# A four-layer network on one core: first loads on two queues, the bias split moved, layer 1's bands prepared in other tiles, q (k^T v) taken two head pairs at a time

## The chip, the cores and the metric

The kernel runs on one NeuronCore of one Trainium2 chip. The metric is the device time of one execution in microseconds (us), lower is better, as the median of several executions. Engines are named as the profile names them: PE is TensorE, DVE VectorE, ACT ScalarE, POOL GpSimd, SP SyncE, which here only issues DMAs. PEld is TensorE's loading of weights, which overlaps its matmuls.

## The reference

The input x has the shape (4, 8, 512, 512): time T, batch B, rows N, columns D. Four layers follow one another, each a residual on a group normalisation of x (two batch entries make one group):

```python
x = x + attention(_gn(x), ...)   # layer 0
x = x + conv13x13(_gn(x), w)     # layer 1, one Gaussian kernel per channel, reflected edges
x = x + conv3x3_quantised(_gn(x), weight, bias)   # layer 2
x = x + conv3x3(_gn(x), weight, bias)             # layer 3
```

Layer 0, where the change lies, is a spiking attention with 8 heads of 64 columns:

```python
q = heads(lif(bn(x @ Wq.T)))     # the same for k and v
scores = einsum('tbhnd,tbhmd->tbhnm', q, k) * scale + bias_table[rel]
out = lif(einsum('tbhnm,tbhmd->tbhnd', scores, v))
out = lif(bn((out * gate_scale + gate_shift) @ Wp.T))
```

`lif` runs over the four time steps: a potential is averaged with its input, gives a spike (0 or 1) where it reaches 1, and is then reset. No softmax stands between scores and values. So scores @ v may be taken as q (k^T v), which needs only a 64 x 64 matrix for each head, plus the bias matrix times v. The bias depends on the distance of two rows alone.

## The kernel before

**Layer 0** (`layer0`, L268 to L733) goes through 32 steps, one for each (b, t). What a step needs of the projections is made one step ahead. In the loop over n, `attend` (L533) works on step n, then `project_in` (L518) makes v, k and q of step n+1, in 3 x 4 groups, and `project_out` (L579) for step n is put between them in four groups.

- `attend`: k^T v goes into one PSUM tile (L540) and is cut to the heads' diagonal blocks on DVE as `kvb` (L545). Then, for each pair of heads j = 0 to 3: `pa` = q·kvb (L552, two matmuls of 64 output rows) and `pb` = the bias times v (L560, 24 matmuls, since the bias is kept as three bf16 parts and the 512 rows are contracted in four blocks of 128). Potential and spikes follow on DVE (ACT in the first time step). The spikes of all four pairs, the tile `so`, feed `project_out`.
- `project_in`: a group is four program matmuls in f32, eight instructions. Its PSUM tile is emptied by DVE into potential and spikes.
- PSUM tiles: the pool `ps_mm` has four that projections in and out and small products share; `ps_b` has two for pb; `ps_1` has one for pa and one for k^T v and small sums.

**The start.** ACT issues `cols` (batch norm parameters) and `bias_table`; SP issues the first x in four quarters (`xq`, L447), a second x of the same group (`xs`, L438), then the weights of v, k and q in quarters (L308). A group's statistics are made on DVE from both x (L456), summed over partitions by small matmuls (`gps`, L180), and normalise xq, which is then transposed (L505). The weights are scaled on DVE by the batch norm's factors (L359), which PE has spread over the free axis (`ps_free`, L346). Then the first v projection runs.

**Prologue.** Beside the projections of step 0 the kernel prepares what later work needs. `split_bias` (L364) splits the bias table into three bf16 parts on DVE and writes them to DRAM. `prepare_bias` (L380) reads them back as 12 hankel tiles, 448 KB each, over ACT's queue, and ACT turns each into a part of `toep`. `prepare_out` (L401) makes the output weights; it needs the `shift` matmuls (L407). `bands1` (L736) prepares layer 1's band matrix in a scratch tile that takes over a buffer of the pool `state` ("h_p"): it fills the DRAM tensor `band1d` with zeros from SBUF (one DMA, 896 KB by the page), computes 13-wide bands by four matmuls (L769) from the constants `c13` and the taps `w1`, writes them into band1d, and sums the taps by a matmul with ones (L784). The ones are written over the zeros (L782).

**Order.** The program is written in Python order, and a scheduler orders the instructions of each engine by its own estimate of times, within dependencies and the hints `tc.issue_after(op)`. An engine carries out its instructions in that order. A tile's buffer is given to the next tile of the same tag once its readers are done. A DMA from SP or ACT takes one of eight semaphores in turn, and so waits for the DMA eight earlier, whichever of the two queues that was on.

**After layer 0** come layer 1 (`Layer1`, L810) with one band matmul a tile (L843), and layers 2 and 3 (L1037).

Of the kernel before, what the change touches and what calls it, by code (L numbers as in the profile page):

```python
# [35 lines left out]
F32 = mybir.dt.float32  # L36
# [6 lines left out]
PSUM = bass.MemoryType.PSUM  # L43

P = 128
T, B, N, D, H = 4, 8, 512, 512, 8
DH = D // H
NC = N // P
SQ = 32
# [8 lines left out]
PH, NV = 4, D // 4  # L58
W1_IN, W1_OUT = 28, 16
W1_N = N // W1_OUT  # L60
X1_R, X1_U = N + 2 * R1, (D + 2 * R1) // PH
# [68 lines left out]
def network(ctx: ExitStack, tc: tile.TileContext, i: dict, out: bass.AP):  # L130
    nc = tc.nc
# [96 lines left out]
            s, tc, i, x_in, x1d, ident, block, avg, group_stats, st1, norm1, band1d, r1, w_sum, shared  # L228
        )

    nc.vector.tensor_scalar_mul(avg_same, same, 1.0 / n_half)

    def pool(name, bufs=1, **where):
        return tc.tile_pool(name=name, bufs=bufs, reuse_waits="tile", **where)

# [10 lines left out]
    with ExitStack() as s:  # L246
        ps_1 = s.enter_context(pool("ps_2", space=PSUM))
        layer1 = Layer1(
            s, tc, x1d, x2d, avg, group_steps, r1, mr1, st2, m2, r2, most, w_sum, head, ps_1, pool
        )  # L250
        layer1.group(0)
        for g in range(1, G):
            if g == 1:
                with ExitStack() as behind:
                    for op in layer1.started:
                        behind.enter_context(tc.issue_after(op))
                    norm1(G - 1, ps_1)
# [10 lines left out]
def layer0(  # L268
# [2 lines left out]
    nc = tc.nc  # L271
    half_scale = 0.5 / math.sqrt(D)

    ps_mm = s.enter_context(tc.tile_pool(name="ps_mm", bufs=4, space=PSUM))
    ps_b = s.enter_context(tc.tile_pool(name="ps_b", bufs=2, space=PSUM))
    ps_1 = s.enter_context(tc.tile_pool(name="ps_1", bufs=1, space=PSUM))
    wpool = s.enter_context(tc.tile_pool(name="w0", bufs=1))
# [24 lines left out]
    work = s.enter_context(tc.tile_pool(name="work", bufs=1))  # L302


    def load_weights(n, engine):
        rows = i[f"wT_{n}"].rearrange("(q c a) e -> q a c e", c=NC, a=SQ)
        for q in range(P // SQ):
            engine.dma_start(wT[n][q * SQ : (q + 1) * SQ], rows[q])  # L308

    nc.scalar.dma_start(cols.rearrange("p a b -> p (a b)"), i["cols"])  # L310
    bn = cols[:, :16, :].rearrange("p (n s) c -> p n s c", s=4)
# [52 lines left out]
    def split_bias():  # L364

        n_e = n_h // 3
        parts = tc.dram_tile([3, H * n_h], BF16, name="bias_parts")
        src = state.tile([3 * H, n_e], F32, tag="h_o", name="bias_table")
        nc.scalar.dma_start(src, bass.AP(i["table"].tensor, 0, [[n_e, 3 * H], [1, n_e]]))
        part = state.tile([3 * H, 3, n_e], BF16, tag="h_p", name="bias_part")  # L370
        for z in range(3):
            nc.vector.tensor_copy(part[:, z, :], src)
            if z < 2:
                nc.vector.tensor_sub(src, src, part[:, z, :])
        nc.scalar.dma_start(
            bass.AP(parts.tensor, parts.offset, [[n_e, 3 * H], [H * n_h, 3], [1, n_e]]), part
        )
        return parts
# [60 lines left out]
            got.append(xt)  # L439
        return got  # L440

    def load_quarters(b, t):

        xt = xqp.tile([P, N // SQ, P], F32, tag="xq", name=f"xq_{b}_{t}")
        rows = x_in[t, b].rearrange("(j s) (q f) -> q s j f", s=SQ, f=P)
        for q in range(P // SQ):
            nc.sync.dma_start(xt[q * SQ : (q + 1) * SQ], rows[q])  # L447
        return xt

    def as_rows(xt):  # L450
# [82 lines left out]
    def attend(got, t):  # L533
        q, k, v = got["q"], got["k"], got["v"]

        kv = ps_1.tile([P, NC, P], F32, tag="misc", name="ps_kv")
        for j in range(NC):
            cut = slice(j * P, (j + 1) * P)
            for c in range(NC):
                nc.tensor.matmul(  # L540
                    kv[:, j, :], lhsT=k[:, c, cut], rhs=v[:, c, cut],
                    start=c == 0, stop=c == NC - 1,
                )
        kvb = work.tile([P, NC, P], F16, tag="kvb", name="kvb")
        nc.vector.tensor_mul(kvb, kv, block.unsqueeze(1).to_broadcast([P, NC, P]))  # L545
        spikes = work.tile([P, NC, N], F32R, tag="so", name="so")
        for j in range(NC):
            pa = ps_1.tile([P, N], F32, tag="pa", name="ps_a")
            pb = ps_b.tile([P, N], F32, tag="pb", name="ps_b")
            for two in range(2):  # L550
                out = slice(two * DH, (two + 1) * DH)
                nc.tensor.matmul(  # L552
                    pa[out, :], lhsT=kvb[:, j, out], rhs=q[:, j, :], start=True, stop=True
                )
            for c in range(NC):
                u = P * (NC - 1 - c)
                for z in range(3):
                    for two in range(2):
                        h = 2 * j + two
                        nc.tensor.matmul(  # L560
                            pb[two * DH : (two + 1) * DH, :],
                            lhsT=v[:, c, h * DH : (h + 1) * DH],
                            rhs=toep[z][:, h, u : u + N],
                            start=c == 0 and z == 0,
                            stop=c == NC - 1 and z == 2,
                        )
# [8 lines left out]
            nc.vector.scalar_tensor_tensor(w, pb, 0.5, w, op0=ALU.mult, op1=ALU.add)  # L575
            fire(w, h, t, None, spikes[:, j, :])
        return spikes
# [70 lines left out]
    def load(n):  # L648
        if n <= last:
            xs[n] = load_quarters(*steps[n])  # L650
# [18 lines left out]
    a_rows = as_rows_of(a_half.rearrange("p n c -> p (n c)"))  # L669
    c_rows = as_rows_of(c_half[:, :3, :].rearrange("p n c -> p (n c)"))  # L670
    with tc.issue_after(normed):
        load(0)
        statistics(0, 0, 0, as_rows(xs[0]))
        statistics(0, 0, 1, load_x(1, 0, "xs"))
        for n in "vkq":
            load_weights(n, nc.sync)
        bias_parts = split_bias()
    for k in range(NC):
        transpose(0, k)
# [3 lines left out]
    for n in range(-1, last + 1):  # L683
# [39 lines left out]
        if n < 0:  # L723
            with ExitStack() as behind:
                for op in first:
                    behind.enter_context(tc.issue_after(op))
                prepare_bias(bias_parts)
                prepare_out(load_out())
                next_group(n)
                bands1(tc, i, band1d, w_sum, eye, ps_mm, state)  # L730
            for name in "op":
                h_of[name] = state.tile([P, NC, N], F32, tag=f"h_{name}", name=f"h_{name}")
    return head  # L733


def bands1(tc, i, band1d, w_sum, eye, psum, state):  # L736


    nc = tc.nc
    n_s = SHIFTS * PH  # L740
    n_w, n_p = K1 + 2 * (PH - 1), K1 * PH
    scratch = state.tile([P, 2 * P + B * n_w + PH * n_p + B], F32, tag="h_p", name="bands1")
    at = 0

    def part(n_part, n):
        nonlocal at
        at += n
        return scratch[:n_part, at - n : at]
# [14 lines left out]
    nc.vector.memset(zeros, 0.0)  # L763
    rest = band1d.rearrange("p (r m) -> p r m", r=W1_OUT)
    nc.scalar.dma_start(rest, zeros.unsqueeze(1).to_broadcast([K1_P, W1_OUT, P]))

    ps = psum.tile([n_p, P], F32, tag="mm", name="ps_band")
    for f in range(PH):
        nc.tensor.matmul(  # L769
            ps, lhsT=c13[:, f, :], rhs=w1[:, :, f : f + n_s], start=f == 0, stop=f == PH - 1  # L770
        )
# [10 lines left out]
    nc.vector.memset(zeros[:K1, :], 1.0)  # L782
# [565 lines left out]
```

## Time and profile before

| | us |
|---|---|
| three executions | 2902.84, 2903.57, 2905.07 (median 2903.57) |
| the profiled execution | 2902.63 |
| its span, first to last instruction | 2900.8 |
| mean granted TensorE clock | 0.991 |
| layer 0 | from 0 to about 2024 |
| layer 1 | to about 2483 |
| layers 2 and 3 | to 2896 |

Layer 0's steps, from one first v matmul to the next: 81.5 us for the first (with the prologue), 64.2 and 66.2 for the next two, then 61.3 to 63.4. Where DVE's kvb came too late for PE in later steps, PE waited 1.22 us at 718, 0.81 at 1150, 1.71 at 1214 and under 0.6 twice more.

The page is to be read so: busy times are sums over the whole span and say which engine is full; the groups say which line holds the time, and behind the bar how long the engine had been idle just before and on whom it waited. The timeline gives the start of a run of like instructions, its length, and in brackets the idle time ahead of it with its releaser. `ACTq` and `SPq` are the issuing of DMAs; the data moves later.

### The profile page before, as it was taken

The numbers are of one execution on the slowest core, as the hardware profiler recorded it, in microseconds if no ns is written. First come the engines' busy times: TensorE is split into PE (matmuls) and PEld (weight loads), VectorE is DVE, ScalarE is ACT, GpSimd is POOL, SyncE is SP. The second block draws the span as 40 slices with busy tenths as digits, with TensorE's granted clock in tenths as the row PEclk, the third lists the DMA queues.
The fourth block names the chain that finished last, engine by engine and source line by source line (L and its number), as shares of the span: only waits on it lengthen the run. The fifth ranks groups of instructions, "written<-read, shape, count | busy, mean of one in ns | idle before, by whom it ended". The sixth has DMA issues, their size and how long they took to land. (4 is left out here: it accounts for less than half of the span.)

```text
span 2900.8 us, 36559 instructions
## 1 busy us (share of the span) xinstructions
PE 2818.8 (97%) x12868; PEld 1302.5 (45%) x12868; DVE 2183.1 (75%) x3888; ACT 549.2 (19%) x851; POOL 868.8 (30%) x1920
## 2 busy tenths in 40 slices
PE   7999999999999999999999999999999999689999
PEld 3444555545555545455555555445333333223334
DVE  6897788788779878878877886886665665888870
ACT  2200100011010001001000000110111121677774
POOL 2242243333234323333422343332311111232220
PEclk9899999999999999999999999999999999999999
DMA  8433222223222232222222122212877788699975
GB/s 209 115 89 76 59 67 67 74 74 74 59 67 67 77 76 68 59 67 67 75 67 51 45 59 52 52 45 75 221 203 207 209 219 224 157 201 234 224 191 148
DMA packets 326127, 324.01 MB, mean 112 GB/s; under 512 B 21519, under 2 KB 240439, under 8 KB 325831
## 3 DMA queue, kind: packets, MB, share of 16 engines
q1 hardware_dynamic: 263024, 239.48, 34.1%
q0 software_dynamic: 19776, 56.14, 6.0%
q10 hardware_dynamic: 43143, 26.05, 3.1%
q8 instruction: 101, 1.65, 0.3%
q14 instruction: 83, 0.68, 0.1%
HBM read 212.44 MB, written 103.65 MB: 109 GB/s over the span
## 5 line engine op out<-in xcount | busy, mean ns | idle before, releaser
L524 PE MATMUL ps_in<-w_v,xn 128*128 128x512 f32 x1024 | 459.1, 599 | 5.4 <-DVE w_v L359 5.4
L524 PE MATMUL ps_in<-w_kq,xn 128*128 128x512 f32 x1024 | 449.8, 592 | 0.0
L843 PE MATMUL ps_conv<-x,bt 112*64 112x512 f32 x2048 | 445.2, 592 | 0.1
L524 PE MATMUL ps_in<-xn,w_kq 128*128 128x512 f32 x1024 | 444.9, 592 | 0.0
L560 PE MATMUL ps_b<-toep,vtok 128*64 128x512 bf16 x3072 | 367.1, 383 | 0.4 <-DVE v_o L575 0.4
L475 ACT ACTIVATE h_q<-v_q,c_half 128x512 f32<-128x512 f32 x96 | 69.1, 721 | 1473.6 <-DVE v_q L471 893.9
L500 POOL TENSOR_TENSOR h_v<-h_v,c_v 128x512 f32<-128x512 f32 x96 | 121.8, 1269 | 728.0 <-DVE h_v L499 700.1
L587 PE MATMUL ps_out<-wp,so 128*128 128x512 f32 x1024 | 308.7, 444 | 0.0
L609 POOL COPY x1s<-x1s 128x2 f32<-128x2 f32 (+1 forms) x1024 | 226.6, 275 | 273.0 <-DVE x1s L598 273.0
L524 PEld LDWEIGHTS ps_in<-xn,w_kq 128*128 128x128 f32 x1024 | 194.3, 190 | 232.5 <-issue 220.4
L524 PEld LDWEIGHTS ps_in<-w_kq,xn 128*128 128x128 f32 x1024 | 194.3, 190 | 220.7 <-issue 206.2
L524 PEld LDWEIGHTS ps_in<-w_v,xn 128*128 128x128 f32 x1024 | 191.4, 191 | 222.9 <-issue 212.1
L843 PEld LDWEIGHTS ps_conv<-x,bt 112*64 112x64 f32 x2048 | 146.5, 135 | 288.0 <-issue 286.0
L560 PEld LDWEIGHTS <-vtok 128*64 128x64 bf16 x3072 | 176.1, 111 | 155.1 <-issue 5.6
L1249 PE MATMUL ps_conv<-x,band_t 64*64 64x512 f32 x2040 | 242.7, 595 | 0.0
L587 PEld LDWEIGHTS ps_out<-wp,so 128*128 128x128 f32 x1024 | 192.6, 188 | 94.0 <-issue 57.8
L1153 DVE SCALAR_TENSOR_TENSOR x<-ps_conv,inv,x 128x512 f32<-128x512 f32 (+1 forms) x172 | 186.1, 1169 | 46.9 <-PE ps_conv L1146 46.7
L598 DVE SCALAR_TENSOR_TENSOR x1s<-v_p,xr 128x256 f32<-128x256 f32 x256 | 187.6, 773 | 14.6 <-DMA x<-x1s 3.8
L865 POOL DMA_DIRECT2D x<-xo x128 | 71.4, 564 | 330.6 <-ACT xo L850 316.3
L850 ACT ACTIVATE xo<-ps_conv,off 128x512 f32<-128x512 f32 x128 | 87.6, 687 | 430.6 <-PE ps_conv L843 307.4
L500 POOL TENSOR_TENSOR h_k<-h_k,c_k 128x512 f32<-128x512 f32 x96 | 122.0, 1270 | 138.4 <-DVE h_k L499 138.4
L1146 PE MATMUL ps_conv<-xq,band 128*128 128x512 bf16 (+1 forms) x516 | 131.5, 391 | 31.3 <-POOL xq L1129 31.3
(193 smaller groups left out, 3113.8 us busy)
## 6 DMA issues: line engine op xcount, KB each, us to landing
x<-x SPq DMA_DIRECT2D x64, 917.0 KB
x<-x SPq DMA_DIRECT2D x168, 256.0 KB
x<-x1s POOLq DMA_DIRECT2D x128, 262.0 KB, 2.7
xq<-in_x SPq DMA_DIRECT2D x128, 256.0 KB
xr<-in_x SPq DMA_DIRECT2D x128, 256.0 KB
out<-o SPq DMA_DIRECT2D x164, 192.0 KB
xs<-in_x SPq DMA_DIRECT2D x112, 256.0 KB
x<-xo ACTq DMA_DIRECT2D x128, 128.0 KB
```

The lines of the kernel that those rows point to most:

```text
L500: nc.gpsimd.tensor_add(h, h, c_twice[n])
L524: mm = nc.tensor.matmul(ps, lhsT=lhsT, rhs=rhs, start=k == 0, stop=k == NC - 1)
L560: nc.tensor.matmul(pb[two * DH : (two + 1) * DH, :], lhsT=v[:, c, h * DH : (h + 1) * DH], rhs=toep[z][:, h, u : u + N], start=c == 0 and z ...
L587: nc.tensor.matmul(ps, lhsT=so[:, k, c * P : (c + 1) * P], rhs=wpT[z][:, k, :], start=k == 0 and z == 0, stop=k == NC - 1 and z == 1,)
L598: nc.vector.scalar_tensor_tensor(own, v.rearrange("p (g v) -> p g v", g=PH)[:, two, :], 1.0, by_phase[:, two, :], op0=ALU.is_ge, op1=ALU.add,)
L609: nc.gpsimd.tensor_copy(x1[:, f, u : u + n], x1[:, fm, um - n + 1 : um + 1][:, ::-1])
L843: mm = nc.tensor.matmul(ps[q * M1 : (q + 1) * M1, :], lhsT=bt[:, z, :], rhs=xt[:, w0 : w0 + N_PS1, z : z + NV], start=z == 0, stop=z == SH ...
L850: nc.scalar.activation(xo[:, a, :], ps, AF.Identity, bias=off[:, t : t + 1])
L865: engine.dma_start(bass.AP(dst.tensor, dst.offset + (q * n_half * W1_OUT * B + b) * D + f * NV, [[B * D, W1_OUT], [W1_OUT * B * D, n_half] ...
L1146: mm = nc.tensor.matmul(ps[:n_p, :], lhsT=w["band2"][:n_p, j, dx, :n_p], rhs=xq[:, j, dx : dx + PH, :], start=dx == 0, stop=dx == 2,)
L1153: done["DVE"] = nc.vector.scalar_tensor_tensor(own.rearrange("p (v g) -> p g v", g=PH), by_phase(ps[:n_p, :]), w["inv"][:n_p], by_phase(x[ ...
L1249: mm = nc.tensor.matmul(ps[j][b * HALF : (b + 1) * HALF, :], lhsT=band[half, b, dx, :], rhs=x3[half, s0 + j, dx : dx + D], start=dx == 0, ...
```

## The change

- First loads: the quarters 2 and 3 of the first x, and of the weights of v, are issued by ACT; k and q stay on SP. ACT issues `bias_table` behind them.
- The bias split: the three casts go to ACT, the two subtractions to POOL.
- `bands1`: its scratch is a tile of `x1p` (layer 0's output tiles, two buffers), the zeros have the other of the two, and `c13` and the taps are loaded by POOL's queue. It no longer waits for the buffer "h_p".
- `attend`: pa of two pairs of heads is taken one after the other, each behind the last bias matmul of the pairs before (for j = 0 and 1 behind k^T v's last). pa has two PSUM tiles, `ps_mm` three.
- `avg_same`, one scaling of a constant, is made ahead of layer 1's second group.

```diff
@@ network
-    nc.vector.tensor_scalar_mul(avg_same, same, 1.0 / n_half)
...
                     for op in layer1.started:
                         behind.enter_context(tc.issue_after(op))
+                    nc.vector.tensor_scalar_mul(avg_same, same, 1.0 / n_half)
                     norm1(G - 1, ps_1)
@@ layer0
-    ps_mm = s.enter_context(tc.tile_pool(name="ps_mm", bufs=4, space=PSUM))
+    ps_mm = s.enter_context(tc.tile_pool(name="ps_mm", bufs=3, space=PSUM))
@@ load_weights and load_quarters, each with a parameter engines
-            engine.dma_start(wT[n][q * SQ : (q + 1) * SQ], rows[q])
+            engines[q // 2].dma_start(wT[n][q * SQ : (q + 1) * SQ], rows[q])
...
-            nc.sync.dma_start(xt[q * SQ : (q + 1) * SQ], rows[q])
+            engines[q // 2].dma_start(xt[q * SQ : (q + 1) * SQ], rows[q])
@@ split_bias
-            nc.vector.tensor_copy(part[:, z, :], src)
+            nc.scalar.copy(part[:, z, :], src)
             if z < 2:
-                nc.vector.tensor_sub(src, src, part[:, z, :])
+                nc.gpsimd.tensor_sub(src, src, part[:, z, :])
@@ attend
-        for j in range(NC):
-            pa = ps_1.tile([P, N], F32, tag="pa", name="ps_a")
-            pb = ps_b.tile([P, N], F32, tag="pb", name="ps_b")
+
+        def through_kv(j):
+            pa = ps_1.tile([P, N], F32, tag="pa", name="ps_a", bufs=2)
             for two in range(2):
                 out = slice(two * DH, (two + 1) * DH)
                 nc.tensor.matmul(
                     pa[out, :], lhsT=kvb[:, j, out], rhs=q[:, j, :], start=True, stop=True
                 )
+            return pa
+
+        for j in range(NC):
+            if j % 2 == 0:
+                with tc.issue_after(mm.ins):
+                    pas = [through_kv(jj) for jj in (j, j + 1)]
+            pa = pas[j % 2]
+            pb = ps_b.tile([P, N], F32, tag="pb", name="ps_b")
@@ layer0's first loads
-        load(0)
+
+        both = nc.sync, nc.scalar
+        xs[0] = load_quarters(*steps[0], both)
         statistics(0, 0, 0, as_rows(xs[0]))
         statistics(0, 0, 1, load_x(1, 0, "xs"))
-        for n in "vkq":
-            load_weights(n, nc.sync)
+        load_weights("v", both)
+        for n in "kq":
+            load_weights(n, (nc.sync, nc.sync))
         bias_parts = split_bias()
...
-                bands1(tc, i, band1d, w_sum, eye, ps_mm, state)
+                bands1(tc, i, band1d, w_sum, eye, ps_mm, x1p)
@@ bands1
-    scratch = state.tile([P, 2 * P + B * n_w + PH * n_p + B], F32, tag="h_p", name="bands1")
+    scratch = pool.tile([P, PH, X1_U], F32, tag="x1", name="bands1").rearrange("p f u -> p (f u)")
+    zeros = pool.tile([P, PH, X1_U], F32, tag="x1", name="zeros1")
+    zeros = zeros.rearrange("p f u -> p (f u)")[:K1_P, :P]
-    zeros, band = part(K1_P, P), part(n_p, P)
+    band = part(n_p, P)
-    nc.scalar.dma_start(
+    nc.gpsimd.dma_start(
         c13, i["c13"].rearrange("k (f j) -> k f j", f=PH)[:, :, (W1_OUT - 1) * PH :][:, :, :n_p]
     )
-    nc.scalar.dma_start(taps, i["w1"].rearrange("k (c d) -> k c d", c=B))
+    nc.gpsimd.dma_start(taps, i["w1"].rearrange("k (c d) -> k c d", c=B))
```

More of the change, by code (lines that the diff above doesn't have):

```diff
@@ L302, in layer0, with load_weights @@
     work = s.enter_context(tc.tile_pool(name="work", bufs=1))
-    def load_weights(n, engine):
+    def load_weights(n, engines):
         rows = i[f"wT_{n}"].rearrange("(q c a) e -> q a c e", c=NC, a=SQ)
         for q in range(P // SQ):
-            engine.dma_start(wT[n][q * SQ : (q + 1) * SQ], rows[q])
+            engines[q // 2].dma_start(wT[n][q * SQ : (q + 1) * SQ], rows[q])
     nc.scalar.dma_start(cols.rearrange("p a b -> p (a b)"), i["cols"])
@@ L440, in load_x, with load_quarters @@
         return got
-    def load_quarters(b, t):
+    def load_quarters(b, t, engines=(nc.sync, nc.sync)):
         xt = xqp.tile([P, N // SQ, P], F32, tag="xq", name=f"xq_{b}_{t}")
@@ L539, in attend @@
             for c in range(NC):
-                nc.tensor.matmul(
+                mm = nc.tensor.matmul(
                     kv[:, j, :], lhsT=k[:, c, cut], rhs=v[:, c, cut],
@@ L559, in attend @@
                         h = 2 * j + two
-                        nc.tensor.matmul(
+                        mm = nc.tensor.matmul(
                             pb[two * DH : (two + 1) * DH, :],
@@ L733, in layer0, with bands1 @@
     return head
-def bands1(tc, i, band1d, w_sum, eye, psum, state):
+def bands1(tc, i, band1d, w_sum, eye, psum, pool):
     nc = tc.nc
```

## The prediction

> **What bounds the kernel now.** I read the page's engine table first, then the groups by line with their shapes kept apart, then the busy times by stretch, and last the timeline of each stretch that lost something.
>
> ```profile
> PE 2818.8 (97%) x12868; PEld 1302.5 (45%) x12868; DVE 2183.1 (75%) x3888; ACT 549.2 (19%) x851; POOL 868.8 (30%) x1920
> L552 PE MATMUL ps_a<-q,kvb 128*64 128x512 f16 x256 | 55.8, 393 | 11.7 <-DVE kvb L545 10.5
> ```
>
> TensorE is the bound: it is idle for 2900.8 − 2818.8 = 82 us in all. So the change can win only idle time, half-clock time or matmul time; it removes no matmul. The second line says that q·kvb, which the change regroups, waited 10.5 us for kvb over all 32 steps.
>
> ```profile
> 0.00:23.00 23.00, 5.99 (x23) 5.00 (x24) 14.16 (x37) 2.39 (x4) 4.95 (x9) 1.00 0.88 195
> 69.00:104.00 35.00, 28.69 (x181) 18.20 (x181) 23.39 (x43) 15.94 (x23) 0.54 (x1) 0.71 0.55 141
> 104.00:168.00 64.00, 62.80 (x257) 31.51 (x256) 58.94 (x110) 5.45 (x9) 25.86 (x50) 1.00 0.39 100
> 168.00:234.00 66.00, 63.11 (x256) 31.53 (x252) 58.90 (x102) 5.41 (x8) 25.71 (x49) 0.97 0.30 81
> 234.00:296.00 62.00, 61.97 (x256) 31.32 (x252) 44.08 (x78) 1.26 (x2) 15.50 (x41) 1.00 0.28 69
> ```
>
> Columns: length, then PE, PEld, DVE, ACT and POOL busy, the clock, DMA share, GB/s. Layer 0's regular step (last row) leaves TensorE no hole. What can be had lies in the start (17 us idle), the prologue of step 0 (6.3 us idle at clock 0.71) and the first two steps (1.2 and 2.9 us idle, with VectorE busy 59 of 64 to 66 us: it sets their length). The other 50 us or so are in layers 1 to 3, which the change hardly touches.
>
> ```profile
> 22.66 5.94 PE L524 MATMUL ps_in<-w_v,xn 128*128 128x512 f32 x8 [5.35 <-DVE w_v L359]
> ...
> 89.68 0.64 PE L552 MATMUL ps_a<-q,kvb 128*64 128x512 f16 x2 [2.33 <-DVE kvb L545]
> 93.87 1.91 PE L769 MATMUL ps_band<-bands 13*52 13x128 f32 x8 [3.56 <-DMA bands<-in_w]
> 96.75 1.01 PE L560 MATMUL ps_b<-toep,vtok 128*64 128x512 bf16 x3 [0.41 <-DVE v_o L575]
> ...
> 158.06 1.89 PE L560 MATMUL ps_b<-toep,vtok 128*64 128x512 bf16 x16
> 159.78 0.38 PE L552 MATMUL ps_a<-q,kvb 128*64 128x512 f16 x2
> 160.00 2.76 PE L560 MATMUL ps_b<-toep,vtok 128*64 128x512 bf16 x24
> 162.59 0.38 PE L552 MATMUL ps_a<-q,kvb 128*64 128x512 f16 x2
> ...
> 222.48 0.64 PE L552 MATMUL ps_a<-q,kvb 128*64 128x512 f16 x2 [2.89 <-DVE kvb L545]
> 222.91 3.02 PE L560 MATMUL ps_b<-toep,vtok 128*64 128x512 bf16 x16
> ```
>
> **What the Trainium skill says.** "TensorE: Matmul & The Clock Gate", Part 1, has TensorE run at half clock by default and after an idle window of about 3.4 us, until it has been busy as long again. The trace agrees in kind, already for shorter waits: after the 2.89 us at 222.48 sixteen matmuls took 225.76 − 222.91 = 2.85 us, at 158.06 they took 1.72, so the wait cost 1.1 us more than itself. "DMA: Bandwidth & Descriptors", section "Issuing engines are not separate DMA queues", says a second issuing engine saves only the time of issuing. The trace agrees that little else is to be had: the DMA engines are at 0.88 in the first 23 us. The same page's "Queues, rings and completion order" has descriptors of one ring consumed in order; that places the zeros transfer below behind the hankels. "GPSIMD Engine Reference", 4.1, makes a two-input operation about twice VectorE's time; no 24x341 subtraction of GpSimd is in the trace.
>
> **1. Start.** From VectorE go three casts and two subtractions.
>
> ```profile
> 7.75 0.32 DVE L372 CAST bias_part<-bias_table 24x341 bf16<-24x341 f32 x1
> 9.94 2.48 DVE L456 BATCH_NORM_STATS2 st<-xq 128x6 f32<-128x512 f32 x4
> 12.33 2.46 DVE L456 BATCH_NORM_STATS2 st<-xs 128x6 f32<-128x512 f32 x4
> ```
>
> They fill 7.75 to 9.87, ahead of the statistics on which everything to the first matmul (22.66) hangs. If xs is there, the whole 2.1 us are won; the last xs quarter landed at about 11.7 now, and the statistics take it in fourths of 0.62, so at worst 1.5 us are. I take 1.75. The split goes to ScalarE and GpSimd (two subtractions at an estimated 1.0 us, twice 0.50), later than now, but its first reader, a hankel, is issued only at 30.68: hidden. w_v's third and fourth quarters go by ScalarE's queue; their landing (18.6 at the latest) is ahead of the scaling at 21.95 already: nothing.
>
> **2. The zeros transfer, a new wait.** band1d is first filled with zeros, a transfer of 896 KB.
>
> ```profile
> 92.81 0.69 ACTq L765 DMA_DIRECT2D band1d<-bands  x1
> 98.70 0.17 DVE L782 MEMSET bands<- 13x128 f32 x1 [0.92 <-DMA band1d<-bands]
> ```
>
> With its own tile it is issued much earlier, in ScalarE's order right behind the sixth hankel pair, at about 48. The memset that rewrites the zeros with ones then stands on VectorE before k's last potential, and it waits until the transfer has read them. VectorE works in order. Behind the memset stand k's last potential and spikes (1.75 us), the statistics of the next x (8 x 0.61 = 4.84), q's first potential (0.7) and the sum (0.2): 7.5 us, with one wait more 7.75. TensorE asks for that sum now after eleven of q's sixteen matmuls (two instructions of 0.43 us each) in place of thirteen: 65.88 − 1.72 − 1.75, about 62.4. The hankels ahead in the queue had their data from 49 to 55.9; the zeros took 4.0 us alone (94 to 98), so they land between 55 (shared from the start) and 59.5 (wholly behind). I take 58.4: the sum is ready at 66.15 and TensorE waits 3.75, then loses some 1.6 to half clock (1.3 to 2.3 by the case at 222). From 54.5 downwards it would cost nothing.
>
> **3. kvb and the bands in step 0.** kvb's multiply stands on VectorE ahead of the output weights' chain, no longer late behind it: 2.33 goes. c13 and the taps come over GpSimd's queue some 60 us before they are used: 3.56 goes. The 0.41 goes too, with some 0.7 of q·kvb that stretched to 95.71–96.75, and half clock after those waits (89.7 to 98.8), about 1.9. Sum 8.9. The change puts v's two groups for step 1 (6.87 us) into this place as filler; so the first ps_out follows straight on the last bias matmul and needs the last spikes: of b3's 0.69, comparison and write 0.42, and the drain, about 2.0 us of wait. The scaling rows move behind the shift matmuls: they delay the output weights by 1.4 us, which the bias matmuls (7 us at 77) cover.
>
> **4. Steps 1 and 2.** They are VectorE's; it can be early only by its own lead (0.7 to 3 us) and by the waits for TensorE it loses (up to 2.3). Of a gain up to 5 all can pass, of more than that not.
>
> **5. q·kvb by fours, three PSUM tiles.** In a regular step a pair of q·kvb takes 160.00 − 159.78 = 0.22 us, and 24 bias matmuls take 2.59, 0.216 a pair: switching between them costs nothing, so doing it half as often saves nothing. The first q·kvb still stands behind eight bias matmuls and waits for kvb as now. For the bank that the second q·kvb takes, the projections give one up. Over the 512 projection groups of this trace, comparing when VectorE or ScalarE emptied a tile with when the matmul three groups on began, none would have waited: the least slack is 0.27 us with three (4.09 with four). I put it at 0, with 0.1 us a step (3 us) as bound.
>
> **6. avg_same** (0.26 us at 6.83, beside GpSimd's 2.94 us power): 0.
>
> Sum: −1.75 + 3.75 + 1.6 − 8.9 + 2.0 = −3.3 us. The profiled execution took 2902.63 (span 2900.8 and 1.8 around it), 0.9 under the median; so 2899.3 for such a run, and against the median 2903.57 − 3.3 = **2900.3 us**. Ends of the single terms: start −1.5 to −2.1, the zeros 0 to 7.3, step 0 −6 to −7 net.
>
> **Rivals.** *The zeros land early.* If they share the engines with the hankels and land by 54.5, part 2 falls away: −1.75 − 6.9 = −8.65, of which VectorE in steps 1 and 2 may keep 1: **2895.5**. For it: DMA share is 0.81 before 69. Against: one queue, in order, behind 0.9 MB.
> *Three PSUM tiles stall the projections* (the slower side). The slack of 0.27 us is from one step; VectorE's busy steps (53.7 of 61 us) recur. A wait of 0.3 us in each of 31 steps gives −3.3 + 9.3 = +6.0: **2909.6**. It decides from 3.3/31, about 0.11 us a step. For it: drains lag by up to 6.4 us, and three tiles hold 3 x 3.43 us. Against: no group of the trace overlaps.
> *The regrouping pays.* If pairs in fours saved 0.2 us a step, −3.3 − 6.2: **2894.1**. The 0.22 above speaks against.
>
> **How the numbers follow.** My forecast 0.60, early zeros 0.24, PSUM 0.12, regrouping 0.04. What a measurement can tell from no change is 0.2%, 5.8 us: faster means below 2897.8, slower above 2909.4. The forecast's own range, 2896.5 to 2904.5, lies nearly all within it (0.55 of its 0.60), PSUM half. So faster 0.05 + 0.24 − 0.02 + 0.04 = 0.31, slower 0.08, same 0.61. The range 2894 to 2907 leaves out PSUM's worse half and the tail of early zeros, about 0.17.
>
> **What would show it.** Right: the first v matmul at 20.6 to 21.2 in place of 22.66; a VectorE memset near 52 waiting for the transfer of band1d, and TensorE's gps waiting some 4 us near 62 to 66; no wait of 2.33 and 3.56 around 90, one of some 2 us at the first ps_out; regular steps of the same 61.5 us. Wrong: steps of other length (PSUM or regrouping), a gps without a wait (early zeros), or a step 1 that ends no earlier although step 0 does.

## The result and the profile after

The changed kernel takes 2909.14 us (median of 20 runs, 2903.61 to 2912.69). The kernel before took 2903.51 on the same chip (20 runs, 2900.90 to 2905.71). The ratio is 1.0018, with a 95% interval of 1.0012 to 1.0025: 5.6 us slower, where 3.3 us faster was forecast and the range ended at 2907. The profiled execution took 2907.84 us, its span 4.9 us longer than before.

The engine line of the page and the busy times by stretch, for the kernel after. The columns are those of the same view before. The last three rows lie inside the rows above them.

```profile
PE 2816.4 (97%) x12868; PEld 1298.1 (45%) x12868; DVE 2188.5 (75%) x3883; ACT 549.4 (19%) x854; POOL 872.9 (30%) x1924
```

```profile
0.00:23.00 23.00, 5.65 (x22) 4.66 (x22) 10.85 (x28) 3.82 (x7) 7.42 (x12) 1.00 0.99 213
...
69.00:104.00 35.00, 34.77 (x207) 19.24 (x206) 25.68 (x47) 18.41 (x25) 0.67 (x1) 0.91 0.46 131
104.00:168.00 64.00, 55.24 (x205) 26.17 (x205) 58.82 (x104) 4.78 (x7) 28.22 (x50) 0.97 0.39 100
...
234.00:296.00 62.00, 61.97 (x258) 31.44 (x256) 44.78 (x81) 1.89 (x3) 15.51 (x41) 1.00 0.27 69
...
120.00:140.00 20.00, 19.08 (x55) 9.21 (x52) 20.00 (x35) 0.00 (x0) 15.23 (x27) 1.00 0.27 81
160.00:168.00 8.00, 7.83 (x58) 3.85 (x60) 5.17 (x10) 1.35 (x2) 0.00 (x0) 0.79 0.70 123
224.00:230.00 6.00, 3.88 (x24) 1.83 (x26) 4.02 (x8) 1.29 (x2) 0.00 (x0) 0.72 0.82 155
```

TensorE's matmuls cost the same (2816.4 us busy against 2818.8); its idle time grew from 82.0 to 89.3 us. The stretch from 69 to 104, which was to be won, was won: TensorE is busy 34.77 of 35 us at clock 0.91, before 28.69 at 0.71. The next one was lost: 55.24 of 64, before 62.80. VectorE is as busy there as before (58.82), and from 120 to 140 it has no hole at all. The regular step has not moved.

TensorE's timeline after (start, duration, operation, and in brackets the wait ahead of it and what ended it):

```profile
24.36 2.93 PE L523 MATMUL ps_in<-w_v,xn 128*128 128x512 f32 x3 [5.84 <-DVE w_v L358]
...
67.42 0.38 PE L180 MATMUL gps_x<-gsum_x,avg 128*128 128x1 f32 x2 [2.13 <-DVE gsum_x L177]
...
103.58 1.67 PE L594 MATMUL ps_out<-wp,so 128*128 128x512 f32 x6
106.05 0.74 PE L594 MATMUL ps_out<-wp,so 128*128 128x512 f32 x2 [0.80 <-DVE so L468]
107.84 3.70 PE L523 MATMUL ps_in<-w_v,xn 128*128 128x512 f32 x8 [1.05 <-DVE v_v L491]
...
160.17 0.62 PE L551 MATMUL ps_a<-q,kvb 128*64 128x512 f16 x4 [3.80 <-DVE kvb L544]
...
226.12 1.07 PE L551 MATMUL ps_a<-q,kvb 128*64 128x512 f16 x4 [2.74 <-DVE kvb L544]
...
2570.82 1.46 PE L1158 MATMUL ps_conv<-xq,band 128*128 128x512 bf16 x6 [1.92 <-POOL xq L1141]
...
2589.16 1.46 PE L1158 MATMUL ps_conv<-xq,band 128*128 128x512 bf16 x6 [1.73 <-POOL xq L1141]
```

And VectorE's, then ScalarE's, after:

```profile
11.15 2.47 DVE L455 BATCH_NORM_STATS2 st<-xq 128x6 f32<-128x512 f32 x4 [3.45 <-DMA xq<-in_x]
...
60.05 0.17 DVE L794 MEMSET zeros<- 13x128 f32 x1 [5.84 <-DMA band1d<-zeros]
...
95.94 1.29 DVE L430 TENSOR_TENSOR wp_k<-wp_k,wp 128x512 f32<-128x512 f32 x2 [3.92 <-ACT wp L429]
```

```profile
51.13 0.69 ACTq L777 DMA_DIRECT2D band1d<-zeros  x1
...
93.70 1.68 ACT L393 COPY toep<-hankel 128x1792 bf16<-128x1792 bf16 x1 [3.66 <-DMA hankel<-bias_parts]
95.30 1.13 ACT L429 CAST wp<-wp_k 128x512 fp32r<-128x512 f32 x2
```

Five milestones place the loss, each as after against before:

| | before | after | difference |
|---|---|---|---|
| first v matmul | 22.66 | 24.36 | +1.70 |
| first `ps_out` matmul | 111.25 | 103.58 | −7.67 |
| third k^T v (step 2) | 217.55 | 221.35 | +3.80 |
| last k^T v (step 31) | 2012.00 | 2014.77 | +2.77 |
| layers 2 and 3, first matmul to the end of the span | 405.79 | 407.77 | +1.98 |

TensorE is 7.7 us early at the first `ps_out` and 3.8 late a hundred microseconds on. 0.15 more lies in layer 1. From step 3 to step 31 a step takes 61.70 us, before 61.73.

Part of the 7.67 does not come from the waits that the change was to remove. The 32 `shift` matmuls of the prologue, with one output column each, took 6.30 us before and take 3.63 after. The stretch of these matmuls, before and then after, with the columns of above:

```profile
70.80:77.10 6.30, 6.30 (x36) 6.29 (x36) 4.63 (x7) 3.39 (x4) 0.00 (x0) 0.56 0.49 136
```

```profile
73.90:77.60 3.70, 3.70 (x34) 3.63 (x32) 3.47 (x5) 1.49 (x2) 0.20 (x1) 1.00 0.29 107
```

Before, the granted clock was 0.56 there, although TensorE had been busy for all of the 46 us from 23 to 69. After, it was 1.00.

### The profile page after: what moved, and what is told of

It reads as the page before. It is cut to its first block, busy times and chain, and to the rows that moved or that the text cites. A ratio compares the mean times of both kernels' runs of the same rounds, so it can differ in the third digit from the quotient of the medians.

```text
span 2905.7 us, 36550 instructions
## 1 busy us (share of the span) xinstructions
PE 2816.4 (97%) x12868; PEld 1298.1 (45%) x12868; DVE 2188.5 (75%) x3883; ACT 549.4 (19%) x854; POOL 872.9 (30%) x1924
## 5 line engine op out<-in xcount | busy, mean ns | idle before, releaser
L567 PE MATMUL ps_b<-toep,vtok 128*64 128x512 bf16 x3072 | 357.1, 383 | 0.2 <-DVE v_o L582 0.2
```

Of the source, the lines that this page charges most:

```text
L567: mm = nc.tensor.matmul(pb[two * DH : (two + 1) * DH, :], lhsT=v[:, c, h * DH : (h + 1) * DH], rhs=toep[z][:, h, u : u + N], start=c == 0 ...
```

## The experiments

In all of them the kernel before ran on the same chip, and the ratios are to it. `kvb` is the time at which VectorE begins its product in steps 1 and 2; "rest" is layers 2 and 3; "shift" is how long the 32 `shift` matmuls took. Two profiles of one kernel differ in kvb and rest by about 1 us: the kernel before, profiled again, has 158.03, 222.69 and 405.95, the kernel after 160.09, 226.13 and 408.29. A ratio rests on 5 to 21 executions, all other columns on one profile each.

| kernel | ratio (95%) | kvb, step 1 | kvb, step 2 | rest | shift |
|---|---|---|---|---|---|
| before | 1 | 157.08 | 221.74 | 405.79 | 6.30 |
| after | 1.0018 (1.0012, 1.0025) | 159.43 | 225.39 | 407.77 | 3.63 |
| split_only | 0.9998 (0.9990, 1.0006) | 157.80 | 222.62 | 405.62 | 5.82 |
| two_queues_only | 1.0012 (1.0005, 1.0019) | 161.12 | 225.23 | 406.65 | 4.80 |
| bands_only | 1.0032 (1.0020, 1.0045) | 164.44 | 231.73 | 408.51 | 6.08 |
| grouped_only | 1.0011 (1.0004, 1.0017) | 159.03 | 223.67 | 405.92 | 3.73 |
| one_queue | 1.0023 (1.0014, 1.0033) | 160.51 | 227.78 | 408.51 | 5.48 |
| ones_apart | 1.0023 (1.0013, 1.0032) | 158.36 | 224.31 | 408.06 | 3.63 |
| queue_and_ones | 1.0011 (1.0004, 1.0018) | 158.65 | 224.53 | 405.89 | 6.09 |
| zeros_late | 1.0000 (0.9992, 1.0009) | 153.61 | 219.74 | 407.73 | 3.91 |
| zeros_late_ungrouped | 1.0012 (1.0005, 1.0018) | 156.27 | 223.32 | 408.11 | 3.73 |
| zeros_late_turn6 | 0.9999 (0.9991, 1.0007) | 154.57 | 220.79 | 407.09 | 3.73 |
| zeros_late_sp | 1.0009 (1.0000, 1.0017) | 158.69 | 222.78 | 406.72 | 5.77 |
| before_stats_later | 0.9994 (0.9986, 1.0002) | 156.72 | 219.47 | 406.11 | 5.77 |
| late_turn6_stats_later | 0.9982 (0.9974, 0.9991) | 153.19 | 217.59 | 407.44 | 6.24 |
| before_turn10 | 0.9999 (0.9990, 1.0007) | 157.50 | 222.47 | 406.68 | 5.82 |
| before_turn16 | 0.9998 (0.9990, 1.0006) | 154.65 | 219.58 | 406.35 | 3.73 |
| after_turn6 | 1.0017 (1.0010, 1.0023) | 160.54 | 226.62 | 405.77 | 4.92 |

How far one profile can be trusted is shown by before_turn16 (more on it under layers 2 and 3). It is the kernel before with one small load that nothing reads, and TensorE, VectorE and ScalarE carry out the same instructions in the same order as before up to step 2. Its `shift` matmuls had the full clock:

```profile
70.10:73.90 3.80, 3.80 (x36) 3.77 (x36) 3.80 (x6) 1.57 (x1) 0.00 (x0) 0.99 0.56 169
```

Its kvb comes 2.4 and 2.2 us earlier than before, and its ratio is 0.9998. So up to some 2.5 us of a difference in kvb between two profiles may be the clock of this one stretch. The kernel after had the full clock there too, and its kvb is late all the same.

### The first loads: taken back, done alone, and the split alone

```diff
-        xs[0] = load_quarters(*steps[0], both)
+        xs[0] = load_quarters(*steps[0])
...
-        load_weights("v", both)
+        load_weights("v", (nc.sync, nc.sync))
```

> The changed kernel with x, xs and w_v loaded by SP's queue alone, as before. Theory 1 (two queues share the engines, so that xq, first in order before, now lands behind parts of xs and w_v): the first v matmul comes at 20.6 to 21.5 in place of 24.36, xq's statistics start by 8.8. The memset still waits for the zeros, so of these 3 us VectorE keeps 1 to 3: 2906 to 2908. Rival (the later start comes from the bias split or from GpSimd's longer chain): the first v matmul stays at 23.5 to 24.5, time 2909.

The two other kernels are the kernel before with this part of the change, or with the moved split, and nothing else.

> The kernel before with the first x and w_v loaded half by ACT's queue, and nothing else (the bias split stays on VectorE; the scheduler puts it behind the statistics). Theory 2 (VectorE is what all waits for until kvb of step 2, and each of its idle microseconds before that is lost): xq's last quarter lands at about 11 in place of 8.6, the first v matmul comes 1 to 2.5 us later than 22.66, and the time is 1 to 3 us above before. Rival (TensorE's path has slack here and the prologue takes the delay up): within 0.5 us of before.

> The kernel before with the bias split on ACT and GpSimd, and nothing else. Theory 2 (VectorE's time up to kvb of step 2 sets the end): 2.1 us of work go from it, 0.5 at least before the first v matmul (22.2), and 0.5 to 2 us reach the end. Rival (VectorE then waits longer for xs or TensorE in the same place): within 0.5 us of before.

In turn: TensorE's timeline of one_queue at the first v matmul, TensorE's of two_queues_only there and VectorE's at its first statistics, and the same two of split_only:

```profile
22.17 5.00 PE L523 MATMUL ps_in<-w_v,xn 128*128 128x512 f32 x6 [5.35 <-DVE w_v L358]
```

```profile
25.42 2.07 PE L524 MATMUL ps_in<-w_v,xn 128*128 128x512 f32 x2 [6.25 <-DVE w_v L359]
```

```profile
11.80 2.47 DVE L456 BATCH_NORM_STATS2 st<-xq 128x6 f32<-128x512 f32 x4 [3.82 <-DMA xq<-in_x]
```

```profile
22.54 2.07 PE L524 MATMUL ps_in<-w_v,xn 128*128 128x512 f32 x2 [5.36 <-DVE w_v L359]
```

```profile
9.82 2.48 DVE L456 BATCH_NORM_STATS2 st<-xq 128x6 f32<-128x512 f32 x4 [0.79 <-DMA xq<-in_x]
```

With one queue in the changed kernel the first v matmul comes at 22.17 (after: 24.36), with two in the kernel before at 25.42 (before: 22.66). The second queue delays the start by 2.2 to 2.8 us, and put into the kernel before it costs 0.12% by itself. The split gains only 0.1 us: once VectorE was free, it had to wait for xq until 9.82, where before the statistics began at 9.94.

Before, xq stood at the head of one queue, with xs and the weights behind it. Now its second half goes by ScalarE's queue, and SP issues xs from 1.71 on, before from 2.77. That xq is late because it shares the DMA engines with xs is inferred from this order; no line shows which transfer an engine served. The engines moved more in the first 23 us (213 GB/s at a share of 0.99, before 195 at 0.88), but did not bring xq sooner: VectorE waits for it until 11.15.

Yet one_queue gains nothing in all, which was not expected. Its memset still waits 5.85 us, until 58.44, its `shift` matmuls took 5.48 us in place of 3.63, and at kvb its lead is gone (160.51). In the changed kernel the start alone does not set the end.

### The ones in a place of their own, alone and with one queue

```diff
-    zeros = zeros.rearrange("p f u -> p (f u)")[:K1_P, :P]
+    flat = zeros.rearrange("p f u -> p (f u)")
+    zeros, ones = flat[:K1_P, :P], flat[:K1, P : 2 * P]
...
-    nc.vector.memset(zeros[:K1, :], 1.0)
+    nc.vector.memset(ones, 1.0)
```

> The changed kernel, but the ones of bands1 have columns of their own, so that the memset no longer waits for the zeros transfer of band1d. Theory 1 (VectorE sets the pace from the prologue to step 2, and the 5.84 us that the memset waited are passed on): VectorE has no wait at 54 to 60, the gps wait of 2.13 us at 67 goes, kvb of step 2 comes 3 to 5 us earlier, the time is 2904 to 2906. Rival (three PSUM tiles or the regrouping cost the time): kvb of step 2 no earlier, time 2908 to 2910. Rival 2 (the late start alone, +1.7, and the last layers, +2.1, make up the loss): 2908.

> The changed kernel with both of these edits. Theory 1: both gains add, since both lie on VectorE's chain: 2901 to 2903, below the kernel before, with kvb of step 2 waiting under 1 us. Rival (regrouping or three PSUM tiles): 2907 or more. Rival 2 (the last layers are slower in this program for a reason of their own): 2904, with layer 0 ending 2 us earlier than before and the end of the span 0.

VectorE's and TensorE's timelines of ones_apart:

```profile
95.17 1.29 DVE L430 TENSOR_TENSOR wp_k<-wp_k,wp 128x512 f32<-128x512 f32 x2 [4.91 <-ACT wp L429]
```

```profile
159.10 1.07 PE L551 MATMUL ps_a<-q,kvb 128*64 128x512 f16 x4 [3.63 <-DVE kvb L544]
```

The memset's wait of 5.84 us is gone, and the wait for `wp` at the end of the prologue has grown from 3.92 to 4.91: the second wait takes the first one's place, and the time is that of the kernel after, where 2904 to 2906 had been expected. With one queue as well the ratio falls to 1.0011, still above the kernel before. This gain does not show at kvb (158.65, with ones_apart 158.36). In the profile it lies in layers 2 and 3 (405.89 against 408.06), which neither edit touches.

### The bands alone, and the zeros behind the hankels

bands_only is the kernel before with the new `bands1`. zeros_late is queue_and_ones with the zeros transfer issued only after the last hankel's copy:

```diff
-    nc.scalar.dma_start(rest, zeros.unsqueeze(1).to_broadcast([K1_P, W1_OUT, P]))
+    with tc.issue_after(made):
+        nc.scalar.dma_start(rest, zeros.unsqueeze(1).to_broadcast([K1_P, W1_OUT, P]))
```

> The kernel before with the new bands1 alone (scratch and zeros in x1p's tiles, c13 and taps by GpSimd's queue). Theory 2: the zeros transfer stands in ACT's queue ahead of six hankels again; the memset waits some 5 us for it on VectorE, and the last hankel is copied 4 to 7 us later than 87.09, so that the casts of the output weights behind it on ACT hold VectorE up a second time: 2 to 5 us above before. Rival (the waits of 2.33 and 3.56 us that go outweigh it): 1 to 3 us below before.

> The changed kernel with one queue for the first loads, the ones apart, and the zeros transfer issued behind the last hankel's copy. Theory 2: the last hankel is copied by 88 as before, VectorE's wait for wp is under 2 us, and the time is 2 to 4 us below that of the run with one queue and ones apart (2904.7), that is within 1.5 us of before. Rival (the regrouping alone holds the rest of the loss): no better than 2904.

ScalarE's timeline of bands_only, and of zeros_late:

```profile
94.19 1.68 ACT L394 COPY toep<-hankel 128x1792 bf16<-128x1792 bf16 x1
```

```profile
84.09 1.68 ACT L393 COPY toep<-hankel 128x1792 bf16<-128x1792 bf16 x1
85.81 0.69 ACTq L780 DMA_DIRECT2D band1d<-zeros  x1
```

VectorE's of bands_only, and TensorE's of bands_only and of zeros_late:

```profile
60.01 0.17 DVE L784 MEMSET zeros<- 13x128 f32 x1 [7.06 <-DMA band1d<-zeros]
```

```profile
165.18 0.64 PE L552 MATMUL ps_a<-q,kvb 128*64 128x512 f16 x2 [6.55 <-DVE kvb L545]
```

```profile
154.34 0.62 PE L552 MATMUL ps_a<-q,kvb 128*64 128x512 f16 x4 [3.37 <-DVE kvb L545]
...
220.48 1.06 PE L552 MATMUL ps_a<-q,kvb 128*64 128x512 f16 x4 [2.67 <-DVE kvb L545]
```

The last hankel was copied at 87.09 before, at 93.70 after, and at 84.09 with the zeros behind. After, the copy waited 3.66 us for its hankel to land; before, it did not wait for that. ScalarE works in order, so its casts of `wp` behind the copy came late too, and VectorE waited for those, 3.92 us at 95.94. So the zeros transfer has two costs: the memset's wait, and the hankels behind it in ScalarE's queue.

But a wait for `wp` is not new. VectorE's and ScalarE's timelines before, and ScalarE's of bands_only:

```profile
86.69 0.69 DVE L431 TENSOR_TENSOR wp_k<-wp_k,wp 128x512 f32<-128x512 f32 x1 [3.62 <-ACT wp L430]
```

```profile
85.88 0.25 ACT L336 COPY rows<-ps_rows 4x128 f32<-4x128 f32 x1 [5.34 <-PE ps_rows L334]
...
87.09 1.68 ACT L394 COPY toep<-hankel 128x1792 bf16<-128x1792 bf16 x1
```

```profile
92.20 0.26 ACT L336 COPY rows<-ps_rows 4x128 f32<-4x128 f32 x1 [7.12 <-PE ps_rows L334]
```

Before, ScalarE stood at `ps_rows`, a small product of TensorE's, and its casts came late for that reason. In bands_only it stood there for 7.12 us, and its last copy, at 94.19, did not wait for a hankel at all. There the late copy is not shown to come from the zeros.

With one queue for the first loads and both costs gone, zeros_late is level with the kernel before, and its kvb is 5.8 and 5.7 us earlier than after. Up to kvb of step 1 VectorE was busy for 117.3 us and idle for 36.4; after, 116.4 and 43.0; before, 116.0 and 41.1. So this kvb moves with VectorE's idle time; its work hardly differs. Against queue_and_ones, where the place of the transfer is the only edit, kvb is 5.0 and 4.8 us earlier, of which some 2 may be the clock (`shift` 3.91 in place of 6.09), and the ratio falls from 1.0011 to 1.0000.

The late transfer alone does not make kvb early. zeros_late_sp (below) has it as well, and differs from zeros_late only in the queue of c13 and the taps. VectorE's timeline:

```profile
87.00 0.69 DVE L431 TENSOR_TENSOR wp_k<-wp_k,wp 128x512 f32<-128x512 f32 x1 [4.85 <-ACT wp L430]
```

There ScalarE stood at `ps_rows` for 6.57 us, and kvb is at 158.69. So it is shown that the edits of zeros_late together take the loss back. That the hankels behind the zeros are the largest part of it is likely from the ratios, but not shown by itself.

Alone, the bands cost 0.32%, some 9 us where 2 to 5 had been expected, and more than the whole change. The parts do not add up: alone they come to 1.0053 together, the change to 1.0018.

### The regrouping, alone and taken out of zeros_late

```diff
-        for j in range(NC):
-            pa = ps_1.tile([P, N], F32, tag="pa", name="ps_a")
+        def through_kv(j):
+            pa = ps_1.tile([P, N], F32, tag="pa", name="ps_a", bufs=2)
...
+        for j in range(NC):
+            if j % 2 == 0:
+                with tc.issue_after(mm.ins):
+                    pas = [through_kv(jj) for jj in (j, j + 1)]
```

> The kernel before with q·kvb of two head pairs together and three PSUM tiles in ps_mm, and nothing else. Theory 1: regular steps of 61.5 us as before, the time within 1 us of before. Rival (three PSUM tiles stall, or the wait at kvb grows): steps longer by 0.1 to 0.2 us, or larger waits in steps 1 and 2: 2907 to 2910.

> The same with q·kvb one pair at a time and four PSUM tiles as before. Theory 2 with a share of some 3 us for the regrouping (as its run alone had it): 2 to 3 us below the run before this one and 1 to 3 us below the kernel before, with kvb of step 1 waiting under 1 us. Rival (the regrouping costs only through the order of VectorE in the old prologue, which is gone here): the same time as the run before this one.

TensorE's timeline of before, of grouped_only and of zeros_late_ungrouped at step 1's kvb:

```profile
157.81 0.41 PE L552 MATMUL ps_a<-q,kvb 128*64 128x512 f16 x2 [0.64 <-DVE kvb L545]
```

```profile
159.77 0.62 PE L552 MATMUL ps_a<-q,kvb 128*64 128x512 f16 x4 [2.10 <-DVE kvb L545]
```

```profile
157.00 0.64 PE L552 MATMUL ps_a<-q,kvb 128*64 128x512 f16 x2 [7.91 <-DVE kvb L545]
```

Both kernels have a regular step of 61.71 us, so three PSUM tiles stall nothing there. But with the regrouping, which these runs change together with the number of PSUM tiles, the wait for kvb changes in steps 0 to 2. Alone it costs 0.11% (wait 2.10 in place of 0.64). Taking it out of zeros_late costs 0.12% (wait 7.91 in place of 3.37), where a gain of 2 to 3 us had been expected. A part that loses in one prologue and wins in another has no price of its own. Why the order works out so was not followed further.

### Is VectorE the pace? Statistics made later

The statistics of the next group of two batch entries are made ahead, four `bn_stats` a step from the prologue on. In these two kernels they begin three steps later, still ahead of that group's steps: up to step 2 VectorE has 12 `bn_stats`, some 8 us, less to do. (Its busy time up to that kvb fell by less, 2.8 us in the first kernel and 5.9 in the second: other operations took longer.) The first is the kernel before with this edit, the second zeros_late_turn6 (below) with it.

```diff
-            if n >= 0:
-                next_group(n)
+            if n >= 2:
+                next_group(n - 3)
```

> The kernel before with the statistics of the next group (VectorE, L456, from next_group) begun three steps later; all is still computed. If VectorE's work sets the pace up to kvb of step 2: the waits for kvb of 0.64 and 2.89 us go, kvb of step 2 comes 3 to 5 us earlier (217 to 219) and the time is 3 to 5 us below before. If TensorE's path or a transfer sets it: kvb of step 2 no more than 1 us earlier and the time within 1 us.

> The run with late zeros and the DMA of 6 rows, with the same edit. If VectorE's work sets the pace, what TensorE won in the prologue now reaches the end: the waits for kvb (3.4 and 2.7 us) fall under 1 us together, kvb of step 2 at 212 to 215, time 5 to 8 us below that run, 2894 to 2897, and more below before than the edit alone brings there. If not: 2900 to 2902.

TensorE's timeline of before_stats_later, then VectorE's and TensorE's of late_turn6_stats_later:

```profile
220.21 0.41 PE L552 MATMUL ps_a<-q,kvb 128*64 128x512 f16 x2 [0.29 <-DVE kvb L545]
```

```profile
100.86 0.69 DVE L583 SCALAR_TENSOR_TENSOR v_o<-ps_b,v_o 128x512 f32<-128x512 f32 x1 [3.25 <-PE ps_b L568]
```

```profile
153.93 1.06 PE L552 MATMUL ps_a<-q,kvb 128*64 128x512 f16 x4 [2.99 <-DVE kvb L545]
...
218.33 0.62 PE L552 MATMUL ps_a<-q,kvb 128*64 128x512 f16 x4 [0.48 <-DVE kvb L545]
```

In before_stats_later TensorE's wait for kvb of step 2 is 0.29 in place of 2.89, and that kvb comes 2.3 us earlier. That is less than the 3 to 5 us expected, and the ratio of 0.9994 (0.9986 to 1.0002) leaves open whether any of it reaches the end.

In the second kernel kvb of step 2 comes 3.2 us earlier (against zeros_late_turn6) and the wait is 0.48, in zeros_late_turn6 2.78. So VectorE's work sets step 2. In step 1 kvb came only 1.4 us earlier, and the wait of 3 us stays. Before it VectorE itself waits 3.25 us for pb, because TensorE makes v's two filler groups ahead of pb: the two engines wait for one another in turn. How much of step 1 VectorE sets is not settled, since this profile had the low clock at `shift` (6.24 us, zeros_late_turn6 3.73). The second kernel is the only one here that beats the kernel before clear of noise, by 0.18% (0.09 to 0.26). Its 2899.1 us miss the 2894 to 2897 expected.

### Layers 2 and 3

> The run with the late zeros, and c13 and the taps over SP's queue in place of GpSimd's. If two more DMAs on GpSimd's queue make the last layers slower (about +2 us from the first matmul of layer 2 to the end in most runs that have them), that stretch is back at 406 and the time is 2 us below the run with late zeros, 1 us below before: 2902. If not: 407.5 to 408.5 and 2904.

> The kernel before with one more small DMA on GpSimd's queue near its start, of 10 rows, into a tile that nothing reads. If the DMA engines of GpSimd's later transfers go on from where the last one ended (c13 and the taps have 13 rows each, 26 in all, 10 beyond 16), this turns them as the change does: 408 us from the first matmul of layer 2 to the end, time 2 us above before. Rival (the last layers' 2 us have another cause): 405.8 to 406.7, time as before.

> The same with 16 rows, a full turn: 405.8 to 406.5 us and the time of before under the theory of turned engines. If any further DMA on GpSimd's queue does it, 408 here too.

> The changed kernel with one more DMA of 6 rows on GpSimd's queue, unread, so that 26 + 6 = 32 rows make two full turns. Theory of turned engines: 405.8 to 406.5 us from the first matmul of layer 2 to the end and 2907, 2 us below the changed kernel; kvb of step 2 as in it (225 to 226). Rival: 407.8 to 408.5 and 2909.

> The run with late zeros and the same DMA of 6 rows. Theory of turned engines: 2 us below the run with late zeros, that is 1 us below the kernel before. Rival: as the run with late zeros, 0 to 1 us above before.

The change hardly touches these layers, yet their length goes with the queue of c13 and the taps. In eight profiles these two loads, and nothing more, are added to GpSimd's queue; seven of the eight, both of the kernel after among them, have 407.7 to 408.5 us, and queue_and_ones has 405.89. The seven profiles with nothing added to that queue have 405.6 to 406.7. zeros_late_sp is one of these, with both loads on SP's queue and 406.72; its ratio is 1.0009, though 1 us less than before had been expected. The theory was that two transfers of 13 rows turn that queue's choice of DMA engines for all its later transfers. A small load of 10 or 16 rows was put into that queue of the kernel before, one of 6 rows (13 + 13 + 6 = 32) into the kernels after and zeros_late:

```diff
+    turn = wpool.tile([P, 8], F32, name="turn")
+    nc.gpsimd.dma_start(turn[:10], i["c128"][:10, :8])
```

before_turn10 has 406.68 and a ratio of 0.9999 (0.9990, 1.0007), before_turn16 406.35 and 0.9998 (0.9990, 1.0006): no 2 us. after_turn6 has 405.77, but a ratio of 1.0017 (1.0010, 1.0023), as after; zeros_late_turn6 407.09. The theory is not borne out. The trace shows only the place, waits for GpSimd's xq of 1.92 and 1.73 us near 2571 and 2589, where before had 0.80 and 0.64 near 2568 and 2581. The cause of these 2 us stays open.

## Why the prediction was wrong

Against the profiled execution, −3.3 us were forecast and +5.2 came. By its steps:

- **1, the start (−1.75 forecast, +1.70 measured): wrong in sign.** The Trainium skill, "DMA: Bandwidth & Descriptors", section "Issuing engines are not separate DMA queues", has transfers of all engines interleave on the same DMA engines. The prediction took from that section only that a second queue gains little. It put the loss at nothing: if transfers interleave, xq, the urgent one, can now share the engines with xs. The times agree, with the statistics 1.2 us later. The gain failed as well: a VectorE free of the split could start earlier only if xq was there, and on one queue xq came at 9.82.
- **2, the zeros (mechanism right).** The memset waited, until 60.05 (58.4 forecast), and TensorE's sum followed 7.4 us after it, as worked out. TensorE waited 2.13 in place of 3.75, since it came some 3 us later itself. Left out were the six hankels behind the zeros in the same queue. The last one's copy waited 3.66 us for it, and through ScalarE the wait at `wp` came at 95.94 in place of 86.69.
- **3, step 0 (right, too small).** The waits of 2.33 and 3.56 are gone. The first `ps_out` was to be 3.3 us earlier by the sum of steps 1 to 3, and is 7.67. The wait there is 0.80, and 1.05 at the next v (about 2.0 forecast). 2.67 of the surplus is the clock at the `shift` matmuls. The prediction charged half clock only to waits, and here no wait went ahead of it; this part was not foreseen.
- **4, steps 1 and 2: the step that failed.** "Of a gain up to 5 all can pass, of more than that not." From the first `ps_out` to the last k^T v nothing was to be lost; 10.4 us were (−7.67 to +2.77). That VectorE's work can hold these steps was right, and is shown for step 2. The term that was wrong is "its own lead (0.7 to 3 us)": VectorE had no lead. The change had made it wait at 11.15 and 60.05, the wait for `wp` had only moved, and the waits that it lost did not outweigh these. Up to kvb of step 1 it was idle for 43.0 us in place of 41.1 and busy for 116.4 in place of 116.0, so this kvb came 2.35 us later than before, and the next one 3.65. TensorE's gain was only a longer wait, 3.80 in place of 0.64, with half clock after (0.79 and 0.72 in the last two rows of the windows). So the prediction's own sign, "a step 1 that ends no earlier although step 0 does", is what came. zeros_late shows it from the other side: with 36.4 us of VectorE's idle time, kvb is 5.8 us earlier than after. That VectorE alone sets step 1 is not shown.
- **5 and 6 (0 forecast).** Right for regular steps; wrong for the regrouping in steps 0 to 2. Of `avg_same` no effect was seen.
- **Layers 2 and 3 (0 forecast).** They hold +1.98 of the profile's +4.9, and their cause stays open. Step 4 accounts for the layer 0 part alone.
- **The rivals.** "Three PSUM tiles stall the projections" gave 2909.6, near the measured 2909.1, but by chance: its steps were to be 0.3 us longer, and a step takes 61.70 us, before 61.73. Early zeros did not come (and −8.65 with 1 kept is 2895.9, not 2895.5); zeros_late, where that wait is gone too, came level with the kernel before. In regular steps nothing speaks for a gain of the regrouping.

## What to carry to other kernels

Where two engines are both busy over nine tenths of a stretch, a gain of one may be worth nothing (here 7.67 us) until the other's own landmarks are worked out. List every wait that the change adds to that second engine, and every wait that it takes away, and carry the engine's times, not its lead, to the point where the first needs it. An urgent load that is moved in part to an empty queue can come later than at the head of one queue (here 11.15 in place of 9.94). A large transfer that is not urgent can delay smaller ones behind it in its queue (3.66 us at the last hankel), and through an engine that works in order on what they bring it reaches other engines. Before a stage's length is given a cause, read its granted clock: the same 32 matmuls took 6.30 and 3.73 us. Edits that shift an order have no price of their own; try them together with the order they will meet.

## What was not expected of the hardware

VectorE's instructions stretch beside GpSimd's. VectorE's and GpSimd's timelines after:

```profile
125.54 0.60 DVE L605 SCALAR_TENSOR_TENSOR x1s<-v_p,xr 128x256 f32<-128x256 f32 x1
...
126.15 1.62 DVE L605 SCALAR_TENSOR_TENSOR x1s<-v_p,xr 128x256 f32<-128x256 f32 x1
```

```profile
125.61 1.67 POOL L499 TENSOR_TENSOR h_v<-h_v,c_v 128x512 f32<-128x512 f32 x1 [1.14 <-DVE gbuf_x L191]
```

The first of the two took 0.60 us; it began ahead of the GpSimd operation. The second began while that one ran, and took 1.62; the GpSimd operation ends at 127.28, 0.5 us before it does. Layer 0 has 256 operations of this line. The 90 that began while a GpSimd addition of two tiles was running took 1.13 us in the median, the other 166 all took 0.60 to 0.63. The Trainium skill, "SBUF — State Buffer", section "Who interferes with whom", has a VectorE instruction with two SBUF inputs contend with a GpSimd instruction that reads SBUF; the trace agrees. In the sum it decides little here (58.82 us busy from 104 to 168, before 58.94), but VectorE's busy time in a full stretch is partly such waiting, and not all work.

TensorE's clock was half not only after waits. Before, it was 0.56 at the 32 `shift` matmuls, with no wait over 0.25 us ahead of them; in before_turn16 the same matmuls had 0.99. What decides this was not followed.

The split's two subtractions took 0.82 and 1.15 us on GpSimd, 0.50 on VectorE; 1.0 was forecast.
